# Moving statistics, distances and scales in the opening text of a three-layer graph network

## The chip, the cores and the metric

The kernel runs on one core of a Trainium2 chip. The metric is device time in microseconds (us) of one execution, given as the median of several. A core has five engines with a queue each: TensorE (PE, whose weight loads are shown apart as PEld), VectorE (DVE), ScalarE (ACT), GpSimd (POOL) and SyncE (SP, which here only issues transfers). An engine works through its own queue in order, and waits where an instruction needs another engine's result or a transfer.

## The reference

Node features x (2500 x 256) are normalized by row and passed through relu; three layers of edge convolution over 80,000 edges (sorted by destination) follow; the four feature sets are multiplied by parts of Wf and added to x.

```python
h = jnp.maximum(_layernorm(x, axis=-1), 0.0)
# layer, three times:
m = jnp.concatenate([xi, xj - xi], axis=-1) @ W + b      # xi = x[dst], xj = x[src]
s = jax.ops.segment_sum(m, dst, num_segments=N)
h = relu(s / jnp.maximum(cnt, 1.0)[:, None])
# end
x = x + jnp.concatenate([h0, h1, h2, h3], axis=-1) @ Wf + bf
```

## The kernel before

The 2500 nodes lie in 20 tiles of 128 rows; two neighbouring tiles are a pair q (0 to 9). Because the sum over edges commutes with the product, a layer is z = h @ W, then a product of z with the matrix of edge counts. The kernel builds that matrix on the chip from the sorted edges. Edges are cut into 417 windows of 6 destinations, four blocks of 128 windows; a window's edges are spread over partitions, compared with the numbers 0 to 127 (source within its tile) and with a number of tile and destination, and TensorE multiplies the two 0/1 matrices to counts.

The text has a head (until about 62 us) and then the three layers. In the head nothing is left to a scheduler: a string `order` lists short names, `perform` calls each one's function in turn, and every instruction is issued through a wrapper (`InOrder`) that keeps the order of the calls on its engine. So the string is the order of each engine's queue, and all of these instructions carry the wrapper's line, L282, in the profile; they are told apart by the tiles that they write and read. A digit after a name is a pair, a block or a group:

- `st q`: statistics of both tiles of pair q on VectorE (`st`, `mv`). `rs g`, `sq g`, `sc g`: for a group g of pairs, variance plus 1e-5 (VectorE), root (ScalarE), reciprocal and offset (`rs`, `off`, VectorE). The groups are pairs 0; 1; 2 and 3; 4 to 7; 8 and 9.
- `N q`: normalize the pair in place in `acc` (pair 0 on VectorE and ScalarE, pair 1 on ScalarE, all others on GpSimd). `T q`: transpose it (TensorE, `turned`); `R q`: relu of that into `hT` (ScalarE).
- `Z q`, `F q`: product of the pair with W's lower half and with Wf (TensorE, `pz`). `H`, `L`: high and low part of z (`zh` on ScalarE, `zl` on VectorE). `G q`: the product with Wf to `acc` (ScalarE). `V9`: adds the bias on the last tile (VectorE, `zf`).
- `pk`, `sg`, `se`: find each window's first edge (TensorE, ScalarE, VectorE: `start_i`); `se0` for block 0, `se1` for blocks 1 to 3. `ge i`: two gathers of block i's edges, destinations `ed` and sources `es` (issued by GpSimd).
- `ka i`: source within its tile (`lo_i`, VectorE), the edge's distance from the window's first destination (`away`, ScalarE), and a correction of half of it (`away`, VectorE). `kb i`: second key (`es` or `hi_i`, and `kn`, VectorE). `km i`: first key (ScalarE). `kt i`: both turned by TensorE; `k1`, `k2`: copies of it (ScalarE) to `key_m`, `key_n`.
- `B b`: comparisons for counting step b (VectorE, `one_m`, `one_n`; from B1 on, one call serves two steps, so B2 and B4 issue nothing). `C b`: the counts (TensorE, `bank`), which need a free one of two banks; `E b`: copy to `a` (ScalarE), which frees the bank.

GpSimd's queue in the head is ge0, N6, N5, N7, ge1, N9, ge2, N8, ge3, N3, N2, N4. Loads of x come in four pieces: tiles 0 and 1; 2 to 5; 6 to 11 (the only one on ScalarE's queue); 12 to 19. SyncE's queue then loads parts of W and Wf.

Of the kernel before, what the change touches and what calls it, by code (L numbers as in the profile page):

```python
# [10 lines left out]
AF = mybir.ActivationFunctionType  # L11
# [302 lines left out]
def by_windows(ctx: ExitStack, tc: tile.TileContext, x, src, dst, Ws, bs, Wf, bf, out, missing):  # L314
    nc = tc.nc
    PE, DVE, ACT, POOL, SP = nc.tensor, nc.vector, nc.scalar, nc.gpsimd, nc.sync
    PEo, DVEo, POOLo, ACTo, SPo = (InOrder(tc, e) for e in (PE, DVE, POOL, ACT, SP))
# [19 lines left out]
    N1 = NT * KEEP  # L337
# [45 lines left out]
    away = early.tile([P, WG, CAP], BF16, name="away")  # L383
# [12 lines left out]
    lim = const.tile([P, WG], F32, name="lim")  # L396
    below = const.tile([P, WG], F32, name="below")
# [113 lines left out]
    first = pp.tile([P, 1], F32, name="first")  # L511
    after = pp.tile([P, 1], F32, name="after")
    behind = pp.tile([P, WG * P], F32, name="behind")
    pick = pp.tile([P, WG * P], F32R, name="pick")
# [7 lines left out]
    edges = [None] * WG  # L522
# [47 lines left out]
    def search(i, j):  # L570
        sl = slice(i, j)
        DVEo.tensor_add(base[:, 0, sl], base[:, 0, sl], base[:, 1, sl])
        DVEo.tensor_scalar(start_f[:, sl], row[:, sl], float(R), float(HR + P * R - MORE - CAP), op0=OP.mult, op1=OP.add)
        DVEo.scalar_tensor_tensor(start_f[:, sl], base[:, 0, sl], -0.5, start_f[:, sl], op0=OP.mult, op1=OP.add)
        DVEo.tensor_scalar(start_i[:, sl], start_f[:, sl], 0.0, float(E - CAP), op0=OP.max, op1=OP.min)
# [17 lines left out]
    parts = {}  # L593

    def key_parts(i):
        es, ed = edges[i]
        lo_i = pw.tile([P, CAP], I32, name="lo_i")
        DVEo.tensor_scalar(lo_i, es, P - 1, None, op0=OP.bitwise_and)

        ACTo.activation(away[:, i, :], ed, AF.Relu, bias=below[:, i:i + 1])  # L600
        DVEo.scalar_tensor_tensor(away[:, i, :P], away[:, i, :P], most if i == 0 else float(KEEP), away[:, i, :P],
                                  op0=OP.is_le, op1=OP.mult)
        parts[i] = [lo_i]

    def key_low(i):
        km = pw.tile([P, CAP], BF16, name="km")
        ACTo.copy(km, parts[i][0])
        parts[i][0] = km
# [18 lines left out]
    def key_copy(i, q):  # L627
        n = min(P, NW - i * P)
        to = (key_m, key_n)[q]
        ACTo.copy(to[:, i * P:i * P + n, :, :].rearrange("p n j r -> p j n r"),  # L630
                  parts[i][:, q * CAP:(q + 1) * CAP].rearrange("p (j n) -> p j n", j=CH)[:, :, :n]
                  .unsqueeze(3).to_broadcast([P, CH, n, REP]))
# [226 lines left out]
    def layer(l, g, a, own, PE=PE, ACT=ACT):  # L859
# [41 lines left out]
        "dstr": lambda: ACTo.copy(dst_r[:, MORE:], dst_i),  # L901
        "pk": lambda i: pick_half(i // 10, i % 10), "sg": lambda i: count_half(i // 10, i % 10),
        "se": lambda i: search(*((0, 1), (1, WG))[i]), "ge": get_edges,
        "ka": key_parts, "km": key_low, "kb": key_high, "kt": key_turn,
        "k1": lambda i: key_copy(i, 0), "k2": lambda i: key_copy(i, 1),
        "io": small_numbers, "ws": lambda: DVEo.tensor_sub(ws[0][0], ws[0][0], ws[0][1]),
        "st": stats, "rs": lambda g: spread(*groups[g]), "sq": lambda g: roots(*groups[g]),
# [4 lines left out]
        "warm": keep_warm,  # L912
    }
    order = """
        warm8 lim io first next dstr st0 rs0 sq0 pick sc0 warm7 N0 pk00 sg00 pk01 st1 T0 pk11 R0 sg01 st4 rs1 sq1 Z0 pk30 se0
        sg11 sc1 pk20 N1 st5 sg30 ge0 T1 st6 R1 F0 sg20 pk21 st7 pk10 H0 F1 rs3 st3 sq3 sc3 G0 st9
        L0 sg21 N6 pk31 ka0 kb0 Z1 N5 st8 N7 G1 T6 rs4 sg10 sg31 km0 T5 se1 kt0 R6 H1 st2 F6 sq4 sc4 k10 k20
        rs2 Z6 ge1 L1 T7 B0 R5 R7 Z5 B1 C0 B2 ka1 G6 H6 N9 H5 C1 T9 F7 E0 ge2 kb1 R9 sq2 km1 E1 kt1 C2 B3 k21 Z9
        k11 N8 L6 B4 E2 L5 C3 B5 C4 T8 E3 E4 C5 V9 R8 E5 ge3 ka2 H9 sc2 Z7 H7 F8 G7 B6 N3 N2 ka3 km2 T2 R2 km3
        kb2 C6 T3 kb3 B7 L7 kt2 Z2 B8 B9 L9 E6 C7 k22 k12 kt3 H2 N4 E7 B10 k13 k23 Z8 L2 C8 T4 C9 E8  # L920
        C10 H8 E9
        F9 B11 B12 C11 G8 E10 C12 R4 E12 E11 B13 F5 B14 C13 R3 B15 C14 E13 E14 L8 B16 Z3 G9 B17 C15 C16 H3 E15
        G5 B18 F3 C17 E16 C18 F4 E17 B19 C19 Z4 L3 G3 B20 E18 C20 B21 F2 E19 B22 H4 E20 L4 G4 B23 G2 B24 ws
# [29 lines left out]
    C1 = 1.0 + 1.0 / E12  # L953
# [480 lines left out]
def gnn_kernel(tc: tile.TileContext, x, src, dst, Ws, bs, Wf, bf, out):  # L1434
    nc = tc.nc
    with tc.tile_pool(name="flag", bufs=1) as flag:
        missing = flag.tile([1, 1], I32, name="missing")
        tc.mark_branch_hint_location("again", "LikelyTaken",
                                     engines=[getattr(mybir.EngineType, e) for e in ("PE", "DVE", "Activation")])
        by_windows(tc, x, src, dst, Ws, bs, Wf, bf, out, missing)  # L1440
        again = nc.values_load(missing, min_val=0, max_val=1)
        with tc.If(again > 0, label="again"):
            general(tc, x, src, dst, Ws, bs, Wf, bf, out)
# [28 lines left out]
```

## Time and profile before

| | us |
|---|---|
| median of 3 runs | 475.29 (475.0 to 475.76) |
| the profiled execution | 475.97 |
| its span, first to last instruction | 474.0 |
| PE busy | 462.7 |
| PEld busy | 365.3 |
| DVE busy | 380.5 |
| ACT busy | 310.6 |
| POOL busy | 42.6 |

The granted clock of TensorE is 0.998 of full speed over the span. Times in the profile count from the span's start. "x8" is a number of instructions; "[0.81 <-POOL acc L282]" says that the engine was idle for 0.81 us ahead of the row and that a GpSimd instruction writing `acc` ended that. A row joins equal instructions that follow each other.

### The profile page before, as it was taken

What the parts mean: (1) busy time and instruction counts of PE and PEld (TensorE: products, weight loads), DVE (VectorE), ACT (ScalarE), POOL (GpSimd) and SP (SyncE); (2) the same over time, 40 slices, a digit from 0 to 9 for tenths busy, and PEclk for the clock granted to TensorE, in tenths of its full rate; (3) what the DMA queues carried; (4) which work ended last, traced back from release to release, by engine and by line L of the source; (5) the groups of instructions that cost most, each with busy time, mean ns of one, the idle gap of its engine ahead of it and who ended that gap; (6) DMA issues with size and microseconds to landing.
All of it is one profiled execution on the core that took longest, in us unless ns stands there. A gap on an engine that the chain in (4) does not pass through costs nothing.

```text
span 474.0 us, 7362 instructions
## 1 busy us (share of the span) xinstructions
PE 462.7 (98%) x2739; PEld 365.3 (77%) x2739; DVE 380.5 (80%) x699; ACT 310.6 (66%) x543; POOL 42.6 (9%) x66
## 2 busy tenths in 40 slices
PE   7999999999999999999999999999999999999994
PEld 3787888788778878877887877877788787688694
DVE  7988988799898873499987847876999687569794
ACT  4877677686664541378769857775777797497430
POOL 2674014300101001000000000000000000000000
PEclk9999999999999999999999999999999999999999
DMA  8320073991733707532178552010213955220024
GB/s 277 90 56 1 1 157 66 187 215 35 158 63 69 152 0 152 124 100 75 46 235 310 176 174 62 28 44 5 83 44 97 360 177 176 87 88 0 1 73 147
DMA packets 21775, 52.07 MB, mean 110 GB/s; under 512 B 1943, under 2 KB 12134, under 8 KB 21734
## 3 DMA queue, kind: packets, MB, share of 16 engines
q1 hardware_dynamic: 14950, 33.93, 21.9%
q0 software_dynamic: 5856, 16.51, 18.2%
q10 hardware_dynamic: 928, 1.11, 0.7%
q8 instruction: 22, 0.36, 0.3%
q14 instruction: 19, 0.16, 0.1%
HBM read 36.08 MB, written 15.46 MB: 109 GB/s over the span
## 4 chain that ended last, share of the span: by engine, by line
PE 88%; DVE 5%; POOL 3%; DMA 2%; issue 1%; ACTq 0%; DVEq 0%; POOLq 0%
PE bank L282 84%; PE pz L282 3%; DMA acc<-in_x_dram 2%; DVE acc L282 2%; POOL acc L282 1%; DVE st L282 1%; POOL es L282 1%; POOL ed L282 1%; DVE staged L282 1%; DVE tmp L282 0%; DVE zl L282 0%; DVE mv L282 0%; PE turned L282 0%; DVE kn L282 0%; DVE rs L282 0%
## 5 line engine op out<-in xcount | busy, mean ns | idle before, releaser
L282 ACT CAST block<-staged 128x1008 fp32r<-128x1008 bf16 x120 | 117.8, 1031 | 17.0 <-DVE staged L282 6.3
L282 PE MATMUL bank<-block,zh 128*128 128x504 f32 (+1 forms) x200 | 83.7, 419 | 0.0
L282 PE MATMUL bank<-a,zh 128*128 128x504 f32 (+1 forms) x200 | 81.7, 409 | 0.0
L282 ACT CAST a<-bank 128x480 fp32r<-128x480 f32 (+1 forms) x105 | 54.5, 561 | 39.0 <-PE bank L282 37.2
L282 PE MATMUL bank<-a,zl 128*128 128x504 f32 (+1 forms) x200 | 77.8, 389 | 0.0
L282 PE MATMUL bank<-block,zl 128*128 128x504 f32 (+1 forms) x200 | 77.3, 387 | 0.0
L282 DVE TENSOR_TENSOR one_m<-iota_m,key_m 128x2048 bf16<-128x2048 bf16 (+2 forms) x55 | 64.3, 1169 | 9.9 <-PE bank L282 9.7
L282 PE MATMUL bank<-block,sh 128*128 128x504 f32 x160 | 68.9, 431 | 0.0
L282 PE MATMUL bank<-block,staged 128*128 128x512 f32 (+1 forms) x288 | 63.5, 371 | 0.3 <-DVE staged L282 0.2
L282 PE MATMUL bank<-block,sl 128*128 128x504 f32 x160 | 62.6, 391 | 0.0
L282 PEld LDWEIGHTS bank<-block,staged 128*128 128x128 f32 x288 | 49.2, 188 | 11.4 <-DVE staged L282 1.6
L282 DVE TENSOR_TENSOR one_n<-iota_n,key_n 128x960 bf16<-128x960 bf16 (+2 forms) x110 | 51.4, 509 | 0.0
L282 DVE TENSOR_TENSOR block<-staged 128x1008 fp32r<-128x1008 bf16 x40 | 46.9, 1205 | 5.5 <-PE bank L282 4.2
L282 PEld LDWEIGHTS <-one_m 128*128 128x128 bf16 x834 | 37.4, 97 | 13.6 <-issue 7.6
L282 PEld LDWEIGHTS bank<-block,zh 128*128 128x128 f32 x200 | 37.6, 188 | 10.8 <-issue 2.5
L282 PEld LDWEIGHTS bank<-block,zl 128*128 128x128 f32 x200 | 37.6, 188 | 10.6 <-issue 3.5
L282 PE MATMUL bank<-one_n,one_m 128*128 128x120 bf16 x834 | 44.7, 204 | 0.1
L282 PEld LDWEIGHTS bank<-a,zh 128*128 128x128 f32 x200 | 37.8, 189 | 6.3 <-issue 0.2
L282 PEld LDWEIGHTS bank<-a,zl 128*128 128x128 f32 x200 | 37.8, 189 | 6.3 <-issue 0.2
L282 DVE TENSOR_TENSOR staged<-staged 128x1008 bf16<-128x1008 bf16 x40 | 27.1, 679 | 17.3 <-ACT block L282 16.9
L282 PE MATMUL pz<-wbf,hT 128*128 128x256 f32 x160 | 38.7, 387 | 0.5 <-DMA wbf<-in_L_gnn_Wf_dram 0.2
L282 PEld LDWEIGHTS bank<-block,sh 128*128 128x128 f32 x160 | 30.1, 188 | 10.4 <-issue 3.5
(163 smaller groups left out, 616.4 us busy)
## 6 DMA issues: line engine op xcount, KB each, us to landing
staged<-a_dram SPq DMA_DIRECT2D x52, 504.0 KB, 4.5
a_dram<-a POOLq DMA_DIRECT2D x20, 630.0 KB, 10.8
out_dram<-acc SPq DMA_DIRECT2D x19, 128.0 KB, 1.9
acc<-in_x_dram POOLq DMA_DIRECT2D x3, 640.0 KB
wbf<-in_L_gnn_Wf_dram SPq DMA_DIRECT2D x4, 256.0 KB, 12.6
acc<-in_x_dram SPq DMA_DIRECT2D x1, 896.0 KB, 9.8
acc<-in_x_dram ACTq DMA_DIRECT2D x1, 768.0 KB
wbf<-in_L_gnn_W_dram SPq DMA_DIRECT2D x3, 256.0 KB, 7.4
```

The source lines that it names most:

```text
L282: return self.tc.keep_in_program_order(call(*args, **kwargs))
```

## The change

Only the string and one function are touched. The distance leaves `key_parts` and becomes a step of its own, `aw`. In the string, (1) `st2` (tiles 4 and 5) goes to the place of `st4`, ahead of `rs1`; `st4` goes behind `N1`; (2) `aw` stands directly ahead of `ka` for blocks 0 and 1, ahead of `E2` for block 2 and ahead of `km2` for block 3; (3) `sc2` (tiles 4 to 7) goes from behind `ka2` to between `L6` and `L5`; `N2` goes ahead of `N3`; (4) around these, `ka2`, `kb2`, `km2` and `kb3` come sooner, `C6` goes ahead of `F8`, and `T3` follows `T2` with no counting step between them on TensorE. Each engine issues as many instructions as before.

```diff
     def key_parts(i):
-        es, ed = edges[i]
+        es = edges[i][0]
         lo_i = pw.tile([P, CAP], I32, name="lo_i")
         DVEo.tensor_scalar(lo_i, es, P - 1, None, op0=OP.bitwise_and)
-
-        ACTo.activation(away[:, i, :], ed, AF.Relu, bias=below[:, i:i + 1])
         DVEo.scalar_tensor_tensor(away[:, i, :P], away[:, i, :P], most if i == 0 else float(KEEP), away[:, i, :P],
                                   op0=OP.is_le, op1=OP.mult)
         parts[i] = [lo_i]
+
+    def find_away(i):
+        ACTo.activation(away[:, i, :], edges[i][1], AF.Relu, bias=below[:, i:i + 1])
...
-        "ka": key_parts, "km": key_low, "kb": key_high, "kt": key_turn,
+        "aw": find_away, "ka": key_parts, "km": key_low, "kb": key_high, "kt": key_turn,
...
-        warm8 lim io first next dstr st0 rs0 sq0 pick sc0 warm7 N0 pk00 sg00 pk01 st1 T0 pk11 R0 sg01 st4 rs1 sq1 Z0 pk30 se0
-        sg11 sc1 pk20 N1 st5 sg30 ge0 T1 st6 R1 F0 sg20 pk21 st7 pk10 H0 F1 rs3 st3 sq3 sc3 G0 st9
-        L0 sg21 N6 pk31 ka0 kb0 Z1 N5 st8 N7 G1 T6 rs4 sg10 sg31 km0 T5 se1 kt0 R6 H1 st2 F6 sq4 sc4 k10 k20
-        rs2 Z6 ge1 L1 T7 B0 R5 R7 Z5 B1 C0 B2 ka1 G6 H6 N9 H5 C1 T9 F7 E0 ge2 kb1 R9 sq2 km1 E1 kt1 C2 B3 k21 Z9
-        k11 N8 L6 B4 E2 L5 C3 B5 C4 T8 E3 E4 C5 V9 R8 E5 ge3 ka2 H9 sc2 Z7 H7 F8 G7 B6 N3 N2 ka3 km2 T2 R2 km3
-        kb2 C6 T3 kb3 B7 L7 kt2 Z2 B8 B9 L9 E6 C7 k22 k12 kt3 H2 N4 E7 B10 k13 k23 Z8 L2 C8 T4 C9 E8
+        warm8 lim io first next dstr st0 rs0 sq0 pick sc0 warm7 N0 pk00 sg00 pk01 st1 T0 pk11 R0 sg01 st2 rs1 sq1 Z0 pk30 se0
+        sg11 sc1 pk20 N1 st4 st5 sg30 ge0 T1 st6 R1 F0 sg20 pk21 st7 pk10 H0 F1 rs3 st3 sq3 sc3 G0 st9
+        L0 sg21 N6 pk31 aw0 ka0 kb0 Z1 N5 st8 N7 G1 T6 rs4 sg10 sg31 km0 T5 se1 kt0 R6 H1 F6 sq4 sc4 k10 k20
+        rs2 Z6 ge1 L1 T7 B0 R5 R7 Z5 B1 C0 B2 aw1 ka1 G6 H6 N9 H5 C1 T9 F7 E0 ge2 kb1 R9 sq2 km1 E1 kt1 C2 B3 k21 Z9
+        k11 N8 L6 B4 sc2 aw2 E2 L5 C3 B5 C4 T8 E3 E4 C5 V9 ka2 ge3 kb2 R8 E5 H9 aw3 km2 Z7 N2 N3 C6 ka3 kb3 H7 F8 G7 B6 T2 R2
+        km3 T3 E6 B7 L7 kt2 Z2 B8 B9 L9 C7 k22 k12 kt3 H2 N4 E7 B10 k13 k23 Z8 L2 C8 T4 C9 E8
```

## The prediction

> **What bounds the kernel now.** I read the page first. Of the engines only TensorE is nearly full:
>
> ```profile
> PE 462.7 (98%) x2739; PEld 365.3 (77%) x2739; DVE 380.5 (80%) x699; ACT 310.6 (66%) x543; POOL 42.6 (9%) x66
> ```
>
> So an edit of the opening text is worth what it takes from TensorE's idle time and nothing else. The whole trace's waits of PE come to few, and the only ones in the stretch that the change touches are 0.7 us in two waits "turned <- POOL acc". Next, the chain that ended last, in order of time, leads through just this place:
>
> ```profile
> 31.93 1.39 POOL es L282
> 33.32 2.77 issue
> 36.09 0.02 POOLq L282
> 36.11 0.03 issue
> 36.15 2.33 POOL acc L282 x4
> 38.48 0.04 issue
> 38.52 0.44 PE turned L282 x2
> ```
>
> GpSimd has issued its last gather at 33.32, is idle for 2.77 us, normalizes tiles 6, 7, 4 and 5 (N3, N2), and only then can TensorE transpose tiles 4 and 5 (T2). From there to the end the chain is nearly all PE. The timeline shows why GpSimd is idle, and what TensorE's weight loads (PEld) do meanwhile; the columns are start, length, engine, operation, and in brackets the idle time before it:
>
> ```profile
> 10.14 0.75 DVE L282 BATCH_NORM_STATS2 st<-acc 128x6 f32<-128x256 f32 x2 [1.05 <-DMA acc<-in_x_dram]
> ...
> 13.79 1.59 PEld L282 LDWEIGHTS pz<-wbf,hT 128*128 128x128 f32 x8 [0.47 <-DMA wbf<-in_L_gnn_Wf_dram]
> ...
> 19.29 1.01 PEld L282 LDWEIGHTS turned<-shift,acc 128*128 128x128 f32 x8
> ...
> 20.79 3.32 PEld L282 LDWEIGHTS pz<-wbf,hT 128*128 128x128 f32 x16 [0.20 <-ACT hT L282]
> ...
> 24.16 2.23 POOL L282 TENSOR_SCALAR acc<-acc,rs,off 128x256 f32<-128x256 f32 x1
> ...
> 29.12 0.20 ACT L282 ACTIVATE rs<-rs 128x4 f32<-128x4 f32 x1
> ...
> 33.70 3.32 PEld L282 LDWEIGHTS pz<-wbf,hT 128*128 128x128 f32 x16
> ...
> 34.91 0.53 ACT L282 ACTIVATE away<-ed,below 128x256 bf16<-128x256 int32 x1
> ...
> 35.47 0.29 DVE L282 SCALAR_TENSOR_TENSOR away<-away 128x128 bf16<-128x128 bf16 x1 [2.04 <-ACT away L282]
> 35.68 0.17 DVE L282 RECIPROCAL rs<-rs 128x4 f32<-128x4 f32 x1
> ...
> 36.15 5.38 POOL L282 TENSOR_SCALAR acc<-acc,rs,off 128x256 f32<-128x256 f32 x6 [2.82 <-DVE off L282]
> ...
> 37.84 0.20 PEld L282 LDWEIGHTS turned<-shift,acc 128*128 128x128 f32 x2 [0.81 <-POOL acc L282]
> ...
> 38.52 0.20 PEld L282 LDWEIGHTS turned<-shift,acc 128*128 128x128 f32 x2 [0.49 <-POOL acc L282]
> ...
> 39.77 1.60 PEld L282 LDWEIGHTS pz<-wbf,hT 128*128 128x128 f32 x8
> ...
> 41.39 0.73 PEld L282 LDWEIGHTS <-one_m 128*128 128x128 bf16 x8
> ```
>
> The scales of tiles 4 to 7 (sc2: the reciprocal at 35.68) have had their square roots since 29.32, but stand on VectorE behind "away" of block 2, which waits 2.04 us for the distance that ScalarE makes at 34.91. TensorE ends product F8's weight loads at 33.70 + 3.32 = 37.02 and waits 0.81 and 0.49 us. The row of 13.79 matters too: from F0 to here TensorE has no pause over 0.44 us, and F0 itself starts when its weights (Wf) land.
>
> **Part by part. The statistics (st2).** st2 takes st4's place and st4 follows sc1; no instruction is added. At 10.14 VectorE waits 1.05 us for tiles 8 and 9. Tiles 4 and 5 came with the load of tiles 2 and 3, whose statistics ran at 8.13, so st2 runs at once and rs1, se0 and sc1 come about 1 us sooner. st4 then starts near 10.9, after its data (10.12). The gain fades there: VectorE has done 0.9 us of st2 where it waited 1.05, so all that follows is 0.15 us sooner, until st2's old place at 20.69 gives 0.9 us more; there sc4 waits for its roots on ScalarE (21.32) and B0 for its keys (22.28, before 22.50), so 0.2 us stays. TensorE gains nothing before F0: N1 and T1 end sooner, but F0 stands at 13.79 for Wf. Value: 0. It does move two transfers: gather ge0 (ed at 11.97, es at 13.47) is issued 0.9 us sooner, next to the loads that F0 waits for. Here a rule speaks against the change: the Trainium skill, DMA: Bandwidth & Descriptors, "Issuing engines are not separate DMA queues", says that transfers of all queues run on the same 16 engines and interleave. The trace agrees that they are busy: 10 to 12 us moves 348 and 328 GB/s, all of it by SP's queue. A gather of 128x256 int32, 0.13 MB, is 0.38 us at that rate; by the rule F0, and with it all of TensorE, could be that much late. By the row, ed's data moved 0.6 us after its issue ended (first in the stretch 13.8 to 15.0; from 13.0 to 13.8 only SP's queue moved), so 0.9 us sooner is about 12.9, when the Wf load, issued before two more weight loads on the same queue, must be nearly through. I take 0, with -0.4 (Wf's last part lands sooner, since the gather's issue is then over) to +0.38 as its ends.
>
> **The distances (aw).** For blocks 0 and 1 nothing moves on ScalarE. For block 2, 0.5 us (34.91: 0.53) goes in before E2, at about 31.1; E2 slips from 31.06 to 31.56 and ends near 32.15. C4 takes over its bank at 32.47 at the earliest (C3's weights at 32.05, plus 0.42): hidden, with 0.3 us to spare; beyond that TensorE pays. E3 waited 1.15 us for TensorE, so the 0.5 us is gone by then. Its data must have landed: by half microseconds, the transfers of ed of block 2 (issued at 26.55) are over at 29.0. Block 3's distance comes after H9, near 35.5 to 36.0, instead of 36.83; with km2 it stands ahead of H7 and G7, which end near 37.45 instead of 36.97, before R2 needs ScalarE (38.3).
>
> **The scales (sc2).** Two instructions, 0.33 us, go between L6 and L5, near 29.8, after the roots. They push L5 and compare B5 from 30.65 to at most 30.98; B5 then ends at 33.13, C5 wants it at 33.28 to 33.40. Hidden, and the 0.2 us from st2 helps. GpSimd's queue stays in order (N8, ge3, N2...), so N2 starts at 33.35 where ge3's issue ends. Four tiles by 0.56 us (36.15: x6, the first three free of others) make N2 end at 34.5 and N3 at 35.6. The second rule against: the Trainium skill, SBUF — State Buffer, "Who interferes with whom": a VectorE instruction with two SBUF inputs and a GpSimd one that reads SBUF exclude each other for the whole instruction. The row of 24.16 bears it out: 2.23 us, beside the compares of B1 (23.74 to 26.12), against 0.56 alone. By the rule at full price the four take 8.9 us; by the row of 36.15, beside "away" and "kn", 0.56 to 0.84 each. From 33.13 to B7 VectorE has only such short work, so I take 0.56 to 0.84: at most 36.7, still ahead of T2.
>
> **TensorE's sum.** C6 moves ahead of F8, T2 and T3 stand together. Z7 33.70 + 1.62 (39.77 to 41.39) = 35.32; C6 0.51 = 35.83; F8 1.62 = 37.45; T2 at 37.47. The trace has the same succession once, T6 T5 kt0 and then a product that waits for the first one's relu: 19.29 to 20.79, 1.50 us with its 0.20 of wait. So Z2 starts at 38.97, not 39.77: 0.80 gained of the 1.30, since R2 between T2 and Z2 is now late by some 0.2. VectorE: keys of block 2 end near 34.7; lo_i of block 3 waits for es (31.93 + at most 3.8 to landing = 35.7), "away" for ScalarE (36.0), then 0.3 + 0.3 + 0.6: B7 starts at 37.25 instead of 39.48 and ends at 39.5. C7 wants it at 38.97 + 1.62 = 40.6. So C7's 0.73 us of weights (0.56 elsewhere), kt3 and C11, which waited a little for VectorE, give 0.18 + 0.05 + 0.04. Total 0.80 + 0.27 = 1.07 us; TensorE has no idle time of note behind, so it reaches the end. Span 474.0 to 472.9; the profiled execution 475.97 to 474.9; that one is 0.68 above the median, so the median goes from 475.29 to 474.2.
>
> **Rivals.** 1 (chance 0.60), as summed: 474.2, own range 473.7 to 474.6. 2 (0.22), the gather pushes Wf, or E2 and B5 use up their 0.3 us: a third to a half of the gain goes back, 474.6. For it: transfers saturated at 11 us; against: the Wf load is older. 3 (0.10), another wait takes the place: block 3's es must be in before B7 now, and each us by which it lands after 36.8 is paid by C7; at 37.9 the gain is zero, 475.3. Against: the longest landing was 3.8 us, and this needs 6.0. 4 (0.08), slower: the compares lock out GpSimd on N2 and N3. At 2.23 us each N3 ends at 33.35 + 8.9 = 42.3; T3 needs it at 37.9, so TensorE stands 4.4 us, 475.29 - 1.07 + 4.4 = 478.6. It decides from an N3 end of 39.0 on. Against: no compare stands between B5 and B7.
>
> **Numbers.** Bound for a difference: 0.2%, 0.95 us (474.34). Case 1 lies below it three times in four (0.45), case 2 one in four (0.05): faster 0.50. The rest of both and case 3: 0.42. Case 4: slower 0.08. The range leaves out case 4 and takes in case 3 and the Wf term's good end: 473.6 to 475.4.
>
> **What would show it.** GpSimd's "acc" run starts near 33.4 with no idle time ahead of it; T2's waits for GpSimd are gone; the product after T3 starts 0.8 us sooner with a wait of some 0.2 on "hT"; the compare after the last "kn" starts 2 us sooner; VectorE has no wait for a load at 10.14; F0 stands at 13.79. Wrong, if F0 has moved, if C4 waits for ScalarE, or if lines of 2 us stand in GpSimd's run before T3.

## The result, and the profile after

| | before | after |
|---|---|---|
| median of 12 runs each, us | 475.11 (474.78 to 475.76) | 473.97 (473.65 to 474.64) |
| ratio, 95% interval | | 0.9977 (0.9969 to 0.9985) |
| profiled execution, us | 475.97 | 473.74 |
| its span, us | 474.0 | 471.8 |

The change saves 1.14 us; the interval makes that 0.7 to 1.5. The forecast was 474.2, which is 1.09 below the median it started from. The two profiled executions lie 2.23 apart, twice as much as the medians, so a reader who subtracts one trace from the other explains a microsecond that the change did not make. More on that below.

Of the changed kernel's page, the line of the engines. TensorE remains the one that is full:

```profile
PE 462.1 (98%) x2739; PEld 365.6 (77%) x2739; DVE 381.3 (81%) x699; ACT 310.7 (66%) x543; POOL 42.5 (9%) x66
```

Of the changed kernel's chain that ended last, in order of time (start, length, what). GpSimd has left it; from the landing of Wf on, the head's part of the chain is TensorE:

```profile
3.74 9.59 DMA wbf<-in_L_gnn_Wf_dram
...
35.52 1.81 PE pz L282 x8
37.33 0.87 PE turned L282 x8
38.45 1.99 PE pz L282 x8
40.45 0.55 PE bank L282 x12
```

Of the changed kernel's timeline (start, length, engine, operation, idle time before it and what ended that), the rows that answer to those shown of before:

```profile
10.99 1.19 POOL L282 DMA_INDIRECT ed<-in_dst_dram,start_i  x1 [7.53 <-DVE off L282]
...
13.38 1.59 PEld L282 LDWEIGHTS pz<-wbf,hT 128*128 128x128 f32 x8 [1.05 <-DMA wbf<-in_L_gnn_Wf_dram]
...
29.17 1.09 POOL L282 TENSOR_SCALAR acc<-acc,rs,off 128x256 f32<-128x256 f32 x2
...
29.70 0.16 DVE L282 RECIPROCAL rs<-rs 128x4 f32<-128x4 f32 x1
...
29.89 0.38 DVE L282 SCALAR_TENSOR_TENSOR off<-mv,rs 128x4 f32<-128x4 f32 x1
...
30.42 0.97 POOL L282 DMA_INDIRECT ed<-in_dst_dram,start_i  x1 [0.16 <-issue]
30.44 0.52 ACT L282 ACTIVATE away<-ed,below 128x256 bf16<-128x256 int32 x1
30.80 1.21 DVE L282 TENSOR_TENSOR one_m<-iota_m,key_m 128x2048 bf16<-128x2048 bf16 x1
...
32.63 0.11 PEld L282 LDWEIGHTS <-one_m 128*128 128x128 bf16 x2
...
32.89 5.60 POOL L282 TENSOR_SCALAR acc<-acc,rs,off 128x256 f32<-128x256 f32 x6
32.95 0.29 PEld L282 LDWEIGHTS <-one_m 128*128 128x128 bf16 x6 [0.21 <-issue]
33.19 1.60 PEld L282 LDWEIGHTS pz<-wbf,hT 128*128 128x128 f32 x8
...
35.28 0.30 DVE L282 TENSOR_SCALAR lo_i<-es 128x256 int32<-128x256 int32 x1 [0.27 <-DMA es<-in_src_dram,start_i]
...
36.44 1.21 DVE L282 TENSOR_TENSOR one_m<-iota_m,key_m 128x2048 bf16<-128x2048 bf16 x1
36.95 1.01 PEld L282 LDWEIGHTS turned<-shift,acc 128*128 128x128 f32 x8
...
38.45 1.59 PEld L282 LDWEIGHTS pz<-wbf,hT 128*128 128x128 f32 x8 [0.20 <-ACT hT L282]
...
40.07 0.56 PEld L282 LDWEIGHTS <-one_m 128*128 128x128 bf16 x8
40.59 0.13 PEld L282 LDWEIGHTS <-km 128*128 128x128 bf16 x2
```

The scales' reciprocal runs at 29.70, not 35.68; GpSimd starts its four tiles at 32.89 without idle time; the eight transposes T2 and T3 (36.95) wait for nothing; Z2 (38.45) waits 0.20 us for R2's relu, as forecast; block 3's last compare B7 starts at 36.44. Two rows were not forecast: counting step C5 (32.63) breaks in two, with 0.21 us of idle time inside, and the second of the two scale instructions (`off`, 29.89) takes 0.38 us, where it took 0.16 us in its old place.

**How the time is split.** TensorE bounds the kernel, so the two texts are compared by the time between fixed points of its weight loads: F0 (the first product with Wf), Z9, Z7 and Z2 (those products), `a` (the first load of a layer, where the head ends) and the end of the span. The second trace of the old text is from a repeat (below).

| us | start of F0 | F0 to Z9 | Z9 to Z7 | Z7 to Z2 | Z2 to a | a to end |
|---|---|---|---|---|---|---|
| before, first trace | 13.79 | 16.64 | 3.28 | 6.07 | 21.86 | 412.37 |
| before, second trace | 13.60 | 16.20 | 3.28 | 5.93 | 21.85 | 411.93 |
| after | 13.38 | 16.20 | 3.60 | 5.26 | 21.38 | 411.98 |

Against the first trace 2.2 us are gone, of which 1.24 lie in the first two columns and the last one, where the text before and after is nearly the same. Against the second trace those three columns give 0.17, and what remains is the change: -0.67 at T2, -0.47 behind Z2, +0.32 at C5.

### The profile page after: what moved, and what is told of

The parts are those of the page before. It is cut to its first block, busy times and chain, and to the rows that moved or that the text cites. A ratio compares the mean times of both kernels' runs of the same rounds, so it can differ in the third digit from the quotient of the medians.

```text
span 471.8 us, 7365 instructions
## 1 busy us (share of the span) xinstructions
PE 462.1 (98%) x2739; PEld 365.6 (77%) x2739; DVE 381.3 (81%) x699; ACT 310.7 (66%) x543; POOL 42.5 (9%) x66
## 4 chain that ended last, share of the span: by engine, by line
PE 93%; DVE 3%; DMA 2%; SPq 1%; issue 0%; DVEq 0%
PE bank L282 85%; PE pz L282 7%; DMA wbf<-in_L_gnn_Wf_dram 2%; DVE acc L282 2%; PE turned L282 1%; SPq L282 1%; DVE staged L282 1%; DVE tmp L282 0%; DVE zl L282 0%; DVEq L282 0%
```

## The experiments

Each was timed beside runs of the kernel before on the same chip. The first batch (the changed kernel again, the statistics alone, all but the statistics, scales behind B5) had 33 such runs with a median of 474.99 us; the second (the old text again, scales alone, distances alone, Wf sooner) 33 with 474.81; the third (the remaining four) 17 with 475.44. Ratios are to those.

### Both texts again

No edit: the changed kernel twice more, and the old text as if it were a new kernel.

> The changed kernel once more, for a second trace. In the first, TensorE's text had gained 0.41 us at F0, 0.42 us at kt1 and 0.81 us between Z7 and Z2. Theory 1 (all three come from the change): F0 starts near 13.4, no wait ahead of kt1, Z2 near 38.5, median 1.1 to 1.8 us under the kernel before. Theory 2 (F0 and kt1 scatter from one execution to the next): one or both are back near 13.8 and 0.44 us, and only the piece from Z7 to Z2 (5.26 us) is as in the first trace; median 1.1 us under the kernel before.

> The changed kernel a third time, on the chip of the three before, as their standard. F0 between 13.4 and 13.8, 16.20 us to Z9, 3.4 to 3.6 to Z7, 5.26 to Z2, 21.38 to the first layer; 0.8 to 1.1 us under the kernel before.

> The kernel before once more, for a second trace. In its first trace TensorE waited 0.44 us (with what follows 0.43 us of the way from F0 to Z9, 16.64 instead of 16.20 us in all five other traces so far, also in those that keep one part of the old order). If that wait belongs to one execution, the way from F0 to Z9 is 16.2 us here; if it belongs to the old order as a whole, it is 16.6. From Z7 to Z2: 5.9 to 6.1 us with two waits for GpSimd.

Measured: the changed kernel 473.94 us, ratio 0.9980 (0.9971 to 0.9989), and 473.95, 0.9972 (0.9960 to 0.9984); the old text 474.83, 1.0001 (0.9992 to 1.0010). In all three comparisons the gain is there, by medians 1.05 to 1.49 us.

The first trace of before has a wait that its second one lacks. Its timeline, in kt1, just ahead of Z9:

```profile
29.67 0.11 PEld L282 LDWEIGHTS <-km 128*128 128x128 bf16 x2 [0.44 <-ACT km L282]
```

These 0.44 us are the whole of 16.64 - 16.20 in the table. The interval F0 to Z9 is 16.20 or 16.21 in ten of the 14 traces, old and new texts among them; it is 16.64 in this one, 16.45 and 16.37 in two later ones, and 17.23 where Wf is loaded sooner. So the wait is one of single executions. It matters for the forecast, because everything behind it was read from a TensorE that ran 0.44 us late, and so seemed to leave the other engines more room than they have.

Timeline of the old text's second trace, the wait at T2 and what follows:

```profile
30.41 1.22 DVE L282 TENSOR_TENSOR one_m<-iota_m,key_m 128x2048 bf16<-128x2048 bf16 x1
30.54 1.93 POOL L282 DMA_INDIRECT ed<-in_dst_dram,start_i  x1 [0.16 <-issue]
...
32.66 0.46 PEld L282 LDWEIGHTS <-one_m 128*128 128x128 bf16 x8
...
37.08 0.20 PEld L282 LDWEIGHTS turned<-shift,acc 128*128 128x128 f32 x2 [0.68 <-POOL acc L282]
37.77 0.20 PEld L282 LDWEIGHTS turned<-shift,acc 128*128 128x128 f32 x2 [0.49 <-POOL acc L282]
...
39.01 1.60 PEld L282 LDWEIGHTS pz<-wbf,hT 128*128 128x128 f32 x8
40.64 0.73 PEld L282 LDWEIGHTS <-one_m 128*128 128x128 bf16 x8
41.32 0.12 PEld L282 LDWEIGHTS <-km 128*128 128x128 bf16 x2
```

T2's two waits are here 0.68 + 0.49 = 1.17 us, against 1.30 in the first trace. The timeline of the changed kernel's third trace shows C5's wait again, this time with its cause named:

```profile
32.71 0.11 PEld L282 LDWEIGHTS <-one_m 128*128 128x128 bf16 x2 [0.15 <-DVE one_n L282]
33.03 0.29 PEld L282 LDWEIGHTS <-one_m 128*128 128x128 bf16 x6 [0.20 <-issue]
```

C5 waits for B5's compares. ("issue" names no releaser; but the two pieces start 0.05 us after B5's last two compares have ended, at 32.66 and 32.98 us.) The stretch Z9 to Z7 is 3.60, 3.42 and 3.61 us in the three traces of the changed kernel, against 3.28 in both of the old text: so TensorE loses 0.14 to 0.33 us here.

### The statistics: alone, and all but them

```diff
-        warm8 lim io first next dstr st0 rs0 sq0 pick sc0 warm7 N0 pk00 sg00 pk01 st1 T0 pk11 R0 sg01 st4 rs1 sq1 Z0 pk30 se0
-        sg11 sc1 pk20 N1 st5 sg30 ge0 T1 st6 R1 F0 sg20 pk21 st7 pk10 H0 F1 rs3 st3 sq3 sc3 G0 st9
-        L0 sg21 N6 pk31 ka0 kb0 Z1 N5 st8 N7 G1 T6 rs4 sg10 sg31 km0 T5 se1 kt0 R6 H1 st2 F6 sq4 sc4 k10 k20
+        warm8 lim io first next dstr st0 rs0 sq0 pick sc0 warm7 N0 pk00 sg00 pk01 st1 T0 pk11 R0 sg01 st2 rs1 sq1 Z0 pk30 se0
+        sg11 sc1 pk20 N1 st4 st5 sg30 ge0 T1 st6 R1 F0 sg20 pk21 st7 pk10 H0 F1 rs3 st3 sq3 sc3 G0 st9
+        L0 sg21 N6 pk31 ka0 kb0 Z1 N5 st8 N7 G1 T6 rs4 sg10 sg31 km0 T5 se1 kt0 R6 H1 F6 sq4 sc4 k10 k20
```

This alone on the old text is the first kernel; its reverse on the changed text is the second.

> Only the statistics of tiles 4 and 5 change place with those of 8 and 9; distances and scales as before. Theory 1: the gather of block 0 is issued 0.9 us sooner and F0 starts 0.4 us sooner, so 0.4 us faster. Theory 2: F0 stands where the weights land, within 0.1 us of the kernel before, and the time is that of the kernel before within 0.2 us. In both, the wait of 1.05 us for a load at 10.14 is gone and the two waits of TensorE for GpSimd at T2 (0.81 and 0.49 us) remain.

> The change without its first part: statistics as before, distances, scales and the order around them as after. Theory 1: F0 at 13.8, T2's waits gone, 0.4 us less gain than the full change (about 0.7 us under the kernel before). Theory 2: the full gain, 1.1 us under the kernel before.

Measured: alone 474.75 us, ratio 0.9999 (0.9990 to 1.0008); all but it 474.24, 0.9987 (0.9978 to 0.9996). F0 starts between 13.38 and 13.69 in the eight traces with the statistics early (and Wf's load in its place), and between 13.31 and 13.79 in the five without; neither a gain nor the 0.38 us of loss that shared transfer engines could have cost shows. From F0 to `a` the first takes 47.21 us (old text 47.27), the second 46.25 (changed text 46.26 to 46.46). So the traces show no gain from the statistics in the head. The times leave it open: the first kernel's median is 0.24 us below the old text's, and the second's 0.30 us above the changed one's of the same batch (that is the 0.7 us under the old text that the first theory expected, but without its mechanism, since F0 did not move). Neither difference is clear of noise, so a gain of some 0.3 us from the statistics is neither shown nor ruled out; the rest of the change makes most or all of what was gained.

### The scales alone, the distances alone

Scales alone, on the old text:

```diff
-        k11 N8 L6 B4 E2 L5 C3 B5 C4 T8 E3 E4 C5 V9 R8 E5 ge3 ka2 H9 sc2 Z7 H7 F8 G7 B6 N3 N2 ka3 km2 T2 R2 km3
+        k11 N8 L6 B4 sc2 E2 L5 C3 B5 C4 T8 E3 E4 C5 V9 R8 E5 ge3 ka2 H9 Z7 H7 F8 G7 B6 N2 N3 ka3 km2 T2 R2 km3
```

> The kernel before with one move: the scales of tiles 4 to 7 between L6 and L5, and N2 ahead of N3. Statistics, distances and the places of C6 and the keys as before. My theory, that the wait of GpSimd for the scales is what held T2: T2 and T3 no longer wait for GpSimd, and from Z7 to Z2 some 5.3 us; but VectorE still stands 2 us for the distance of block 2 and then has B7 late, so C7 to C11 keep their small waits, 0.5 us from Z2 to the first layer. 0.5 to 0.8 us faster than before. Rival, that the distances matter in themselves: Z2 then waits for kt2's keys, and 0.2 us or less is left.

Distances alone, on the old text (with `find_away` split off as in the change, and `aw0`, `aw1` directly ahead of `ka0`, `ka1`):

```diff
-        k11 N8 L6 B4 E2 L5 C3 B5 C4 T8 E3 E4 C5 V9 R8 E5 ge3 ka2 H9 sc2 Z7 H7 F8 G7 B6 N3 N2 ka3 km2 T2 R2 km3
+        k11 N8 L6 B4 aw2 E2 L5 C3 B5 C4 T8 E3 E4 C5 V9 R8 E5 ge3 ka2 H9 sc2 Z7 H7 F8 G7 B6 N3 N2 aw3 ka3 km2 T2 R2 km3
```

> The kernel before with one move: ScalarE makes the distance of block 2 ahead of E2. The scales stay behind VectorE's second step of block 2, which then no longer waits, so they come near 34.0 instead of 35.7, N3 and N2 at 34.1 to 36.4, T2 (at 37.0 at the earliest, F8 ahead of it) does not wait. So most of the gain comes back with the scales not moved at all: 0.6 to 0.9 us faster than before. If it is the place of the scales that counts and not what they stood behind, T2 waits as before and nothing is gained.

Measured: scales alone 474.49 us, ratio 0.9993 (0.9984 to 1.0002); distances alone 474.50, 0.9991 (0.9982 to 1.0000). Either one ends the wait at T2: Z7 to Z2 falls from 5.93 to 4.97 and 5.09. That is shorter than the 5.26 of the changed text, with the same steps in it: here C6 stands between T2 and T3, so Z2 does not wait for R2, while in the changed text T3 follows T2 directly and Z2 waits 0.20 us. Yet by the medians each move brings only 0.3 us, less than expected, and neither interval leaves out zero. The timeline of the scales alone:

```profile
36.88 0.29 DVE L282 SCALAR_TENSOR_TENSOR away<-away 128x128 bf16<-128x128 bf16 x1 [0.92 <-ACT away L282]
...
38.42 1.22 DVE L282 TENSOR_TENSOR one_m<-iota_m,key_m 128x2048 bf16<-128x2048 bf16 x1
...
40.26 0.11 PEld L282 LDWEIGHTS <-one_m 128*128 128x128 bf16 x2 [0.36 <-DVE one_n L282]
```

And of the distances alone:

```profile
36.28 0.47 DVE L282 TENSOR_SCALAR lo_i<-es 128x256 int32<-128x256 int32 x1 [2.58 <-DMA es<-in_src_dram,start_i]
...
38.48 1.22 DVE L282 TENSOR_TENSOR one_m<-iota_m,key_m 128x2048 bf16<-128x2048 bf16 x1
...
40.32 0.11 PEld L282 LDWEIGHTS <-one_m 128*128 128x128 bf16 x2 [0.70 <-DVE one_n L282]
```

B7 stays at 38.4 to 38.5 in both: in the one it is held by block 3's distance, which ScalarE makes late, in the other by block 3's sources, which land late. Meanwhile TensorE comes to C7 sooner than before, at Z2's early end, and waits 0.36 and 0.70 us for B7. Z2 to `a` takes 22.06 and 22.41 us where the old text takes 21.85. C5 loses as well: Z9 to Z7 takes 3.62 and 3.42 us instead of 3.28. So part of what is gained at T2 is lost again at C5 and C7. From Z9 to `a` the old text takes 31.06 us, the two single moves 30.65 and 30.91, which is 0.41 and 0.15 less; the whole change takes 30.06 to 30.25, which is 0.8 to 1.0 less and more than their sum. In the whole change B7 starts at 36.4 to 37.1 us, ahead of TensorE. But the whole change is more than these two moves: the keys come sooner too, and C6 and T3 change place (part 4). No kernel had both moves without that, so it is not shown how much of the difference is theirs.

### The scales behind B5

```diff
-        k11 N8 L6 B4 sc2 aw2 E2 L5 C3 B5 C4 T8 E3 E4 C5 V9 ka2 ge3 kb2 R8 E5 H9 aw3 km2 Z7 N2 N3 C6 ka3 kb3 H7 F8 G7 B6 T2 R2
+        k11 N8 L6 B4 aw2 E2 L5 C3 B5 sc2 C4 T8 E3 E4 C5 V9 ka2 ge3 kb2 R8 E5 H9 aw3 km2 Z7 N2 N3 C6 ka3 kb3 H7 F8 G7 B6 T2 R2
```

> The changed kernel with the two scale instructions of tiles 4 to 7 behind compare B5 instead of ahead of L5. In the first trace of the changed kernel counts C5 waited some 0.35 us that they did not wait before. If the 0.33 us of the scales ahead of B5 make that wait, C5 starts 0.39 us after T8, and the time falls by 0.2 to 0.35 us against the changed kernel (1.3 to 1.5 under the kernel before); GpSimd starts N2 near 33.2 and T2 does not wait. If C5 waits for something else, the time is that of the changed kernel.

Measured: 473.83 us, ratio 0.9976 (0.9967 to 0.9985), within 0.1 us of the changed kernel in the same batch (473.94). C5's wait is gone, as it should be: Z9 to Z7 is 3.28 us. But the 0.14 to 0.33 us come back further on. Its timeline:

```profile
30.36 1.21 DVE L282 TENSOR_TENSOR one_m<-iota_m,key_m 128x2048 bf16<-128x2048 bf16 x1
30.48 1.94 POOL L282 DMA_INDIRECT ed<-in_dst_dram,start_i  x1 [0.16 <-issue]
...
36.33 0.41 DVE L282 TENSOR_SCALAR lo_i<-es 128x256 int32<-128x256 int32 x1 [1.77 <-DMA es<-in_src_dram,start_i]
...
37.88 1.22 DVE L282 TENSOR_TENSOR one_m<-iota_m,key_m 128x2048 bf16<-128x2048 bf16 x1
```

With B5 started 0.12 us ahead of it, block 3's first gather keeps GpSimd 1.94 us instead of 0.97; the sources land at 36.31 instead of 35.25; VectorE waits 1.77 us for them; B7 starts at 37.88 instead of 36.44; and Z2 to `a` takes 21.63 us instead of 21.38. So the scales in front of B5 cost C5 a little and buy an earlier landing by it.

### Wf a transfer sooner

Since F0 waits 1.05 us for Wf, this loads it ahead of the last piece of x.

```diff
-    load_x(SPo, *chunks[3])
     load_wf(0, SPo)
+    load_x(SPo, *chunks[3])
```

> The changed kernel with SyncE's load of Wf ahead of the load of x for tiles 12 to 19 (both of them in the same queue). F0 then starts near 12.4 instead of 13.4 to 13.7. Theory A (TensorE alone bounds the head): the whole 1.0 us arrives at the end, 2.1 us under the kernel before. Theory B (behind F0 VectorE and GpSimd have no more than 0.3 us to spare: N9 ends at 26.5 for T9, B1 at 25.8 for C1, B5 at 33.1 for C5): T9, C1 and C5 wait, and 0 to 0.4 us arrives.

Measured: 474.14 us, ratio 0.9987 (0.9978 to 0.9996). That is no better than the changed kernel in any batch (473.94 to 473.97). F0 does start 0.9 us sooner, at 12.49, but F0 to Z9 then takes 17.23 us instead of 16.20. Timeline of this kernel:

```profile
13.37 0.75 DVE L282 BATCH_NORM_STATS2 st<-acc 128x6 f32<-128x256 f32 x2 [0.66 <-DMA acc<-in_x_dram]
...
16.68 0.19 PEld L282 LDWEIGHTS bank<-dst_r,pick 128*128 128x128 f32 x1 [0.58 <-ACT junk L282]
...
27.19 0.20 PEld L282 LDWEIGHTS turned<-shift,acc 128*128 128x128 f32 x2 [0.59 <-POOL acc L282]
...
32.94 0.11 PEld L282 LDWEIGHTS <-one_m 128*128 128x128 bf16 x2 [0.32 <-DVE one_n L282]
```

TensorE, when early, waits for ScalarE, for GpSimd's tiles and for VectorE's compares, and the 0.9 us won at F0 does not reach the end. Why is not settled by this run, since its edit also delays the piece of x that Wf overtakes: that lands at 13.35 us (12.45 in the second trace of the changed kernel), VectorE waits 0.66 us for it, and GpSimd starts N6 at 16.67 us instead of 15.87. So it does not show that the other engines had no slack to follow an earlier F0; part of their lateness is of the edit's own making.

### B7 beside the four tiles

Rival 4 said that compares beside GpSimd's tiles would cost 4.4 us. Here B7 is put there.

```diff
-        k11 N8 L6 B4 sc2 aw2 E2 L5 C3 B5 C4 T8 E3 E4 C5 V9 ka2 ge3 kb2 R8 E5 H9 aw3 km2 Z7 N2 N3 C6 ka3 kb3 H7 F8 G7 B6 T2 R2
-        km3 T3 E6 B7 L7 kt2 Z2 B8 B9 L9 C7 k22 k12 kt3 H2 N4 E7 B10 k13 k23 Z8 L2 C8 T4 C9 E8
+        k11 N8 L6 B4 sc2 aw2 E2 L5 C3 B5 C4 T8 E3 E4 C5 V9 B7 ka2 ge3 kb2 R8 E5 H9 aw3 km2 Z7 N2 N3 C6 ka3 kb3 H7 F8 G7 B6 T2 R2
+        km3 T3 E6 L7 kt2 Z2 B8 B9 L9 C7 k22 k12 kt3 H2 N4 E7 B10 k13 k23 Z8 L2 C8 T4 C9 E8
```

> The changed kernel with compare B7 ahead of ka2, so that VectorE compares from about 33.3 to 35.5, just where GpSimd normalizes tiles 4 to 7. It tests the slower rival of the prediction. If a compare locks GpSimd out, one or two of the four instructions take 1.5 to 2.2 us instead of 0.56, and N3 ends near 36.5 to 37.5 instead of 35.3; T3 wants it at 37.6, so the time moves by less than 0.3 us against the changed kernel. If the full price of the rival held (four of 2.2 us), N3 ends at 42 and the time rises by 4 us. If there is no lock, all four stay under 0.85 us.

Measured: 474.17 us, ratio 0.9975 (0.9965 to 0.9985): the gain is still there. The trace by tile, GpSimd's four instructions on `acc` in this stretch (shortest, median and longest in ns):

```profile
L282 POOL TENSOR_SCALAR acc<-acc,rs,off x4: 557/998/1551, 32.8 to 36.1; 128x256 f32<-128x256 f32 x4
```

Two of the four took 1551 and 1176 ns, two to nearly three times the 557 ns of the first. The slow-down is real, but B7's compares (33.26 to 35.76) cover only two tiles; the fourth ends at 36.91, and T2 needs only the first two. Z7 to Z2 stays at 5.26 us.

### B7 ahead of block 3's keys

B7 does not need block 3, and in the string of the scales behind B5 it waits behind a late landing. So it goes ahead of `ka3`, once with the scales behind B5 as well (`B5 sc2`, and no `sc2` ahead of `aw2`) and once without.

```diff
-        k11 N8 L6 B4 sc2 aw2 E2 L5 C3 B5 C4 T8 E3 E4 C5 V9 ka2 ge3 kb2 R8 E5 H9 aw3 km2 Z7 N2 N3 C6 ka3 kb3 H7 F8 G7 B6 T2 R2
-        km3 T3 E6 B7 L7 kt2 Z2 B8 B9 L9 C7 k22 k12 kt3 H2 N4 E7 B10 k13 k23 Z8 L2 C8 T4 C9 E8
+        k11 N8 L6 B4 sc2 aw2 E2 L5 C3 B5 C4 T8 E3 E4 C5 V9 ka2 ge3 kb2 R8 E5 H9 aw3 km2 Z7 N2 N3 C6 B7 ka3 kb3 H7 F8 G7 B6 T2 R2
+        km3 T3 E6 L7 kt2 Z2 B8 B9 L9 C7 k22 k12 kt3 H2 N4 E7 B10 k13 k23 Z8 L2 C8 T4 C9 E8
```

> The changed kernel with the scales behind B5 and B7 ahead of the keys of block 3. With the scales alone behind B5, C5's wait was gone, but VectorE stood 1.77 us for block 3's sources to land, B7 started at 37.9 instead of 36.7, and TensorE lost 0.25 us between Z2 and the first layer. If that landing is what takes the gain back, B7 ahead of it frees C7 to C11: Z9 to Z7 3.28, Z7 to Z2 5.26, Z2 to the first layer 21.4 us, 0.15 to 0.3 us under the changed kernel. If kt3 now waits for block 3's keys instead, Z2 to the first layer is 21.6 us or more and nothing is gained.

> The changed kernel with B7 alone moved, ahead of the keys of block 3; the scales stay ahead of L5. TensorE's C7 to C11 do not wait in the changed kernel (21.38 us from Z2 to the first layer), so no gain: the time of the changed kernel within 0.1 us. If the landing of block 3's sources costs in some executions only, the times scatter less than those of the changed kernel and the median falls by up to 0.15 us.

Measured: with the scales behind B5 473.98 us, ratio 0.9966 (0.9955 to 0.9977); without 473.90, 0.9969 (0.9957 to 0.9981); the changed kernel in the same batch 473.95. No better version. In the first, both small losses are gone (Z9 to Z7 3.28, Z2 to `a` 21.38), and a third takes their place. Its timeline:

```profile
36.70 0.80 PEld L282 LDWEIGHTS turned<-shift,acc 128*128 128x128 f32 x6
37.96 0.20 PEld L282 LDWEIGHTS turned<-shift,acc 128*128 128x128 f32 x2 [0.47 <-POOL acc L282]
```

With the gather's issue at 1.93 us GpSimd starts its tiles at 33.74, and B7's compares then lie beside them (one tile took 1996 ns); the transposes wait 0.47 us for the last one, and Z7 to Z2 is 5.47 us. In the second kernel Z9 to Z7, Z7 to Z2 and Z2 to `a` are 3.32, 5.26 and 21.38, all at their best or near it, but F0 to Z9 was 16.37 in its trace; its time is the same. Its fourth tile, beside B7, took 2.25 us, and T3 did not wait for it. Four orders (the changed text, the scales behind B5, and these two) end within 0.2 us of each other.

## Why the prediction was right, and where its sum was not

The time (473.97 for 474.2), the sign and the place were right, and so was the mechanism in its main part: the scales come sooner, GpSimd follows, T2 does not wait. Step by step:

- **The statistics, 0.** Right as far as the traces show. F0 stands where Wf lands, at 13.3 to 13.8 in all orders that load Wf in its old place. By time alone some 0.3 us stays open. The gather cost F0 nothing that can be seen, but the rule that transfers of all queues share 16 engines (the Trainium skill, DMA: Bandwidth & Descriptors, "Issuing engines are not separate DMA queues") was not put to the test: the gather was issued a microsecond sooner (10.99 instead of 11.97 us), yet in the changed kernel's trace none of its packets moved before 13.0 us and two before 13.4, so it hardly met the load of Wf. It landed at 15.9 to 16.2 us where it was issued early and at 15.9 to 16.3 where it was not. The forecast's 12.9 us for its data was too early.
- **The distances, hidden.** Right for E2 and C4: E2 starts at 30.86 instead of 30.66, and TensorE runs through C3 and C4 (31.21, 16 loads in 0.89 us) without a wait.
- **The scales, "Hidden".** This step failed. It said that B5 would still be in time for C5, which "wants it at 33.28 to 33.40". That time was read from the one execution in which TensorE was 0.44 us late; in the other trace of the old text C5's loads start at 32.66. The price was too low as well. The scales were put at 0.33 us; from L6's start to B5's they added 0.50 (29.10 to 30.80, against 29.21 to 30.41 in the old text's second trace). In all eight traces with the scales ahead of L5, `off` takes 0.37 to 0.41 us and ends 0.01 to 0.02 us after a tile of N8 on GpSimd; in the other six it takes 0.16. It looks as if it waited for that tile, but that was not tested. C5 waited in all three traces of the changed kernel, for 0.14 to 0.33 us. That the scales do it is shown by the two kernels with them behind B5, where Z9 to Z7 is 3.28 us, and that TensorE's lateness hides it by the two that keep them ahead of B5 but came to Z9 0.17 and 0.25 us late (16.37 and 16.45): 3.32 and 3.28. They are not the only thing that can do it: the distances alone, whose F0 was early (13.31), lost 0.14 us too.
- **GpSimd, four tiles at 0.56 to 0.84.** Right: 0.56, 0.61, 0.70 and 0.72 us from 32.89, done at 35.44. The full price of the lock was rightly left out, since the compares don't lie beside these tiles; where B7's do, a tile takes 1.2 to 2.3 us.
- **T2 to Z2, 0.80.** Against the first trace it is 6.07 - 5.26 = 0.81, with the 0.20 of wait for R2 as forecast. Against the second trace it is 0.67, because T2's waits were 0.13 us shorter there.
- **B7, 2 us sooner, worth 0.27.** Right in kind, under-sized: Z2 to `a` gave 0.47. By rows of the second trace of before and of after, C7 gave 0.68 - 0.52 = 0.16 (0.18 was forecast), kt3 0.36 - 0.19 = 0.17 (0.05), and the stretch from Z8 through C11 0.09 + 0.05 = 0.14 (0.04).

Put right, the sum is 0.67 + 0.47 - 0.26 (the mean of the three waits at C5, 0.32, 0.14 and 0.33) = 0.88 us. The medians say 1.14, 1.05 and 1.49 in three comparisons. The intervals of all three (0.7 to 1.5, 0.5 to 1.4, 0.8 to 1.9) take 0.88 in. In the third the old text ran at 475.44, and what made it slower there was not seen in a trace; a scatter like the 0.44 us at kt1 could do it, but that is only argued. So the forecast came out nearer than its sum deserved, and that was luck: a lost 0.26 us and a gain read 0.20 us too small offset each other.

Of the rivals, the second (E2's or B5's slack used up) did happen, for a quarter of the gain. The third (block 3's landing holds B7) is what the distances alone and the scales behind B5 show: the sources land at 36.3 us in both, and in the latter that costs 0.25 us, though the rival's threshold was 36.8. The fourth had its mechanism right and its count wrong: in the run made for it two tiles, not four, are hit, at 1.55 and 1.18 us. The price of 2.23 us for one tile does occur (2.00 and 2.25 us with B7 ahead of `ka3`), but no order paid it four times.

## What to carry to other kernels

Slack is a difference of two times, and in one trace either may be off by half a microsecond: before an edit is called hidden by 0.3 us, the same rows should be read in a second execution. Where a bounding engine waits twice in a row for different engines, freeing one wait alone can pay little, since it then reaches the next one sooner; the two moves here gave 0.3 us each, and the change that holds both, with the reordering around them, 1.1. And an experiment that moves one transfer ahead of another has moved two: the one that is overtaken has to be read as well. Four orders with different small waits end here within 0.2 us of each other, which suggests that little is left to win from moving these steps about; no order was found that had none of the waits.

## What was not expected of the hardware

The price of a gather's issue on GpSimd goes with the start of a compare on VectorE. Block 3's first gather took 0.97 us in the seven traces in which it started 0.37 or 0.38 us ahead of B5's compare, and also in the first trace of before, where the two started within 0.01 us of each other. It took 1.90 to 1.94 us in the six in which the compare had started 0.11 to 0.15 us before it. In the latter it ends about when B5's compares end (32.47 and 32.51 us in the second trace of the old text). The sources then landed 5.5 to 5.8 us after the gather's start, against 4.8 to 5.1. The Trainium skill (SBUF — State Buffer, "Who interferes with whom") has an exclusive lock that goes to whichever of VectorE and GpSimd issues first, and that fits; but the compare that starts behind the gather keeps its 1.21 us, which such a lock alone would not give. The mechanism was not tested.
